# Two-layer graph attention on one core: the second layer's dense residual steps in two pieces for a node tile, in place of five

## The chip, the cores and the metric

The kernel runs on one core of a Trainium2 chip. A core has a matrix engine (TensorE; PE in the profile, its weight loads as PEld), a vector engine (VectorE, DVE), a scalar engine (ScalarE, ACT), GpSimd (POOL), a queue engine (SyncE, SP), and 16 DMA engines. The metric is the device time of one execution in microseconds (us). Three runs of the kernel before took 1968.49, 1970.66 and 1971.56 us; the median is 1970.66.

## The reference

The input is `x`, 3125 nodes by 768 features, and a graph of 53,125 edges (25,000 in each direction, and one from each node to itself), sorted by destination. A layer norm and a relu are followed by two graph attention layers and the sum with `x`:

```python
def gat_conv(x, edge_index, W, a_src, a_dst, bias, heads, out_ch, concat):
    xl = (x @ W).reshape(n, heads, out_ch)
    e = leaky_relu(alpha_src[src] + alpha_dst[dst], 0.2)
    alpha = softmax of e over the edges of each destination
    out = segment_sum(xl[src] * alpha[:, :, None], dst, num_segments=n)
    return out + bias
...
h0 = x
h = relu(layer_norm(gat_conv(h0, W1, 4 heads of 256))) + (h0 @ Wr1 + br1)
h1 = h
h = layer_norm(gat_conv(h1, W2, 1 head of 768))
h = h + (h1 @ Wr2 + br2)
return x + h
```

The change is in the second layer. Its sums over the edges (`segment_sum`) and its residual product `h1 @ Wr2 + br2` (1024 by 768) are worked on in one stage.

## The kernel before, in words

The nodes are cut into 25 tiles of 128 (the last has 53 rows). The edges of a node tile fill up to 17 slots of 128 edges. The function `sums` (L704) does the sums of a layer. For each node tile it goes through five rounds of 4, 4, 3, 3 and 3 slots. In a round, TensorE multiplies for each slot a weight tile `w` (edges by 32 destinations; the attention value where an edge ends at the destination) with the gathered rows `g` of that slot, and adds into the tile `pa` in PSUM (L830): sixteen recorded matmuls in a round, 32 columns wide, four groups of columns side by side. Then it issues the fetch of the next round: a gather for each slot on GpSimd's queue (L783, rows of layer 2's node table, into one of 26 buffers), a copy of three columns on ScalarE (L787), and `w` on VectorE (L805). After that comes `step(k)` (L715), where `k` counts the rounds from 0.

`step(k)` does two things. First it moves on each running `finish` generator (L726) of the node tiles before: the values `v`, `z` from `pa` (L753), the bias (L1396) and the norm's sums (L486) behind the second round of the next tile, the root on ScalarE (L492) behind the third, L496, L1399 and L1400 behind the fourth, and the store of the output (L1402) behind the fifth. L1400 reads the residual `xr`. Second it adds `pace[k]` to a balance, and calls `next(more)` once for every whole unit in it.

`more` is the dense work of the stage, the residual of node tiles 1 to 24 in order (`ahead_of`, L1340, calling `residual`, L1322; that of tile 0 stands ahead of the stage). For one node tile it has eleven steps. The first eight are two matmuls each into a pair of PSUM tiles `pr` (L1329, 128 by 128 by 384 in fp32; four matmuls in the trace's records), the first of them behind the loads of `h` and `xr` for the node tile two further on (L1309, L1319, SyncE's queue). The ninth is reached through the bias matmuls (L1333), two more are empty, and the call that starts the next node tile begins with VectorE's addition of `pr` into `xr` (L1338). Behind it, in the same call, stands that next tile's first pair of matmuls.

The order of the instructions on TensorE, ScalarE and VectorE is that in which the program writes them (`manual_schedule`, L814); a planner places those of GpSimd and SyncE. So what `pace` sets is after which round of `pa` how much of the dense work stands in TensorE's queue, and with it the additions on VectorE's and the loads on SyncE's.

The pace of layer 2 is one number for all five rounds:

```python
each = (NB - FIRST) * (NK2 + 3) / ((NB - 1.5) * len(ROUNDS))   # 24 * 11 / (23.5 * 5) = 2.2468
```

With it, two or three steps follow every round, 11.23 in a node tile. Over the stage, 62 rounds are followed by two pairs of matmuls, 16 by three, 20 by one and 27 by none (these meet the empty steps, or come when nothing is left); 108 rounds have dense matmuls behind them, the bias ones counted.

Of the kernel before, what the change touches and what calls it, by code (L numbers as in the profile page):

```python
# [33 lines left out]
ROUNDS = [(0, 5, 9, 13), (1, 6, 10, 14), (4, 11, 15), (2, 8, 16), (3, 7, 12)]  # L34
# [9 lines left out]
@with_exitstack  # L44
def preln_gat2_kernel(
    ctx: ExitStack,
    tc: tile.TileContext,
    x, src, dst,
    W1, a_src1, a_dst1, b1, g1, be1, Wr1, br1,
    W2, a_src2, a_dst2, b2, g2, be2, Wr2, br2,  # L50
    out,
):

    pool = ctx.enter_context(tc.tile_pool(name="flag", bufs=1))
    flag = pool.tile([1, 1], I32, name="flag")  # L60
    in_order(tc, x, src, dst, W1, a_src1, a_dst1, b1, g1, be1, Wr1, br1,
             W2, a_src2, a_dst2, b2, g2, be2, Wr2, br2, out, flag)
    other = tc.nc.values_load(flag[0:1, 0:1], min_val=0, max_val=1)
    with tc.If(other > 0):
        any_order(tc, x, src, dst, W1, a_src1, a_dst1, b1, g1, be1, Wr1, br1,
                  W2, a_src2, a_dst2, b2, g2, be2, Wr2, br2, out)
# [3 lines left out]
def in_order(  # L70
# [21 lines left out]
    C2 = W2.shape[1]  # L92
# [36 lines left out]
    table2 = dram.tile([N, C2], F32, name="table2")  # L129
# [51 lines left out]
    def bcast(vec, n, parts=P):  # L181
        return bass.AP(tensor=vec.tensor, offset=vec.offset, ap=[[0, parts], [1, n]])
# [11 lines left out]
    def store_rows(q, dst_, b, t):  # L194
        for o, e in pieces(b):
            q.dma_start(dst_[b * P + o:b * P + e, :], t[o:e])
# [284 lines left out]
    def norm_steps(pool, z, n, apart=1):  # L481
        f = n // 2
        P = z.shape[0]
        st = pool.tile([128, 2, 6], F32, name="bn_st")[:P]
        for i in range(2):
            nc.vector.bn_stats(st[:, i, :], z[:, i * f:(i + 1) * f])  # L486
        mv = pool.tile([128, 2], F32, name="bn_mv")[:P]
        nc.vector.bn_aggr(mv, st)  # L488
        for _ in range(apart):
            yield  # L490
        sd = pool.tile([128, 1], F32, name="bn_sd")[:P]
        nc.scalar.activation(sd, mv[:, 1:2], AF.Sqrt, bias=eps[:P])  # L492
        for _ in range(apart // 2 + 1):
            yield
        rstd = pool.tile([128, 1], F32, name="bn_rs")[:P]
        nc.vector.reciprocal(rstd, sd)  # L496
        norm_steps.found = mv[:, 0:1], rstd
# [348 lines left out]
    with tc.tile_pool(name="m1", bufs=1) as mp:  # L846
# [322 lines left out]
        with tc.tile_pool(name="w2", bufs=1, reuse_waits="tile") as wp, tc.tile_pool(name="e1", bufs=2, reuse_waits="tile") as ep, \  # L1169
# [14 lines left out]
            def later():  # L1184
                for i, members in enumerate(late_in):
                    n = cols_of(i)
                    held = [b for g in late_in[:i] for b in g]
                    while len([b for b in held if b not in gone]) + len(members) > 4:
                        yield
                    for b in members:  # L1190
                        made[b] = ep.tile([128, NK2, P], F32, name="r1l", bufs=4)
                    for m in range(NK2):
                        pm = pp.tile([128, 512], F32, name="pr", bufs=2)
                        for k in range(NK1):
                            nc.tensor.matmul(pm[:, :n], wr1[:, k, m * 128:(m + 1) * 128], loaded[i, k][:, :n],  # L1195
                                             start=(k == 0), stop=(k == NK1 - 1))
                            if m == NK2 - 1:
                                load(i + 1, k)
                            if k == NK1 - 1:
                                for t, b in enumerate(members):  # L1200
                                    r = rows_of(b)
                                    nc.scalar.activation(made[b][:, m, :r], pm[:, t * P:t * P + r], AF.Identity,
                                                         bias=br1_c[:, m:m + 1])
                                    if m == NK2 - 1:
                                        whole.add(b)
                            if k % 2:
                                yield

            more = later()
# [67 lines left out]
    with tc.tile_pool(name="m2", bufs=1, reuse_waits="tile") as mp, \  # L1277
            tc.tile_pool(name="pr2", bufs=1, space=PSUM, reuse_waits="tile") as pr:
        al2 = mp.tile([128, J, 1, NB], F32, name="al2")
        ends2 = mp.tile([128, J, NB, 3], F32, name="ends2")  # L1280
# [59 lines left out]
        def ahead_of(first, end, apart):  # L1340
            load(first)
            load(first + 1)
            for b in range(first, end):
                load(b + 2)
                yield from residual(b, apart)
# [40 lines left out]
        more = ahead_of(FIRST, NB, 3)  # L1386
        each = (NB - FIRST) * (NK2 + 3) / ((NB - 1.5) * len(ROUNDS))

        with tc.tile_pool(name="w3", bufs=1, reuse_waits="tile") as wp, tc.tile_pool(name="e2", bufs=2, reuse_waits="tile") as ep, \
                tc.tile_pool(name="g2", bufs=1, reuse_waits="tile") as gp, tc.tile_pool(name="pg2", bufs=1, space=PSUM, reuse_waits="tile") as pp:  # L1390
            with tc.issue_after(last_hot):
                nc.sync.dma_start(b2_b, bcast(b2, C2))
                nc.sync.dma_start(g2_b, bcast(g2, C2))

            def end2(b, z, share):
                nc.vector.scalar_tensor_tensor(z, z, share, b2_b[:z.shape[0]], op0=OP.mult, op1=OP.add)  # L1396
                yield from norm_steps(ep, z, C2, 1)
                mu, rstd = norm_steps.found
                nc.vector.scalar_tensor_tensor(z, z, mu, g2_b[:z.shape[0]], op0=OP.subtract, op1=OP.mult)  # L1399
                nc.vector.scalar_tensor_tensor(z, z, rstd, xrs[b][:z.shape[0]], op0=OP.mult, op1=OP.add)  # L1400
                yield
                store_rows(nc.scalar, out, b, z)  # L1402

            with tc.issue_after(behind), tc.issue_after(last_hot):
                sums(1, C2, table2, al2, ends2, 26, 1, gp, gp, pp, end2, more, [each] * len(ROUNDS))


@with_exitstack
# [469 lines left out]
```

## Time and profile before

| what | value |
|---|---|
| median of three runs | 1970.66 us |
| profiled execution | 1969.17 us |
| its span | 1967.3 us |
| granted TensorE clock, mean | 0.955 |
| busy, share of the span | PE 91%, PEld 50%, DVE 54%, POOL 46%, ACT 15% |
| stage of layer 2's sums | from 1344 us to some 1955 us of the span |

How to read it: busy is the time in which an engine has an instruction in work. PE and PEld overlap. L numbers are lines of the kernel. In lists of groups, what stands after a bar is the idle time of the engine just ahead of the group's instructions and what ended it; "issue" means that the profile shows nothing that was waited for. In the chain of waits, each row is a start, a length, and the work or wait that filled it. In tables by window the columns are busy us and count for each engine, the granted clock, the share of the DMA engines' time in use, and GB/s.

### The profile page before, as it was taken

What the parts mean: (1) busy time and instruction counts of PE and PEld (TensorE: products, weight loads), DVE (VectorE), ACT (ScalarE), POOL (GpSimd) and SP (SyncE); (2) the same over time, 40 slices, a digit from 0 to 9 for tenths busy, and PEclk for the clock granted to TensorE, in tenths of its full rate; (3) what the DMA queues carried; (4) which work ended last, traced back from release to release, by engine and by line L of the source; (5) the groups of instructions that cost most, each with busy time, mean ns of one, the idle gap of its engine ahead of it and who ended that gap; (6) DMA issues with size and microseconds to landing.
All of it is one profiled execution on the core that took longest, in us unless ns stands there. A gap on an engine that the chain in (4) does not pass through costs nothing. (4 is left out here: it accounts for less than half of the span.)

```text
span 1967.3 us, 34126 instructions
## 1 busy us (share of the span) xinstructions
PE 1794.7 (91%) x12558; PEld 986.9 (50%) x12558; DVE 1058.8 (54%) x3030; ACT 296.9 (15%) x1094; POOL 910.2 (46%) x991
## 2 busy tenths in 40 slices
PE   8999999998779999999999999869988898898896
PEld 5666665665446555565554554464333333333332
DVE  7673436986635566555665564344534444444445
ACT  2122331001202211221111121101100000000000
POOL 2000101112354666566666655134666666666662
PEclk9999999998889999999999998958989999999999
DMA  7834447775598999999999999576999999999984
GB/s 243 268 103 139 128 149 196 172 177 167 209 408 326 390 390 387 385 383 408 404 386 385 385 349 378 206 240 197 321 329 325 332 329 322 332 335 327 336 300 141
DMA packets 179889, 574.86 MB, mean 292 GB/s; under 512 B 32767, under 2 KB 55033, under 8 KB 179588
## 3 DMA queue, kind: packets, MB, share of 16 engines
q0 software_dynamic: 109552, 414.44, 59.1%
q1 hardware_dynamic: 65770, 147.77, 21.6%
q10 hardware_dynamic: 4394, 10.39, 1.3%
q8 instruction: 103, 1.69, 0.3%
q14 instruction: 70, 0.57, 0.1%
HBM read 503.27 MB, written 73.85 MB: 293 GB/s over the span
## 5 line engine op out<-in xcount | busy, mean ns | idle before, releaser
L783 POOL DMA_INDIRECT g<-table,idx_s x832 | 816.1, 981 | 557.4 <-issue 201.4
L830 PE MATMUL pa<-g,w 128*32 128x256 f32 (+2 forms) x5868 | 520.3, 433 | 61.2 <-issue 46.7
L830 PEld LDWEIGHTS pa<-g,w 128*32 128x32 f32 x5868 | 202.8, 111 | 344.5 <-issue 227.4
L1329 PE MATMUL pr<-wr,h 128*128 128x384 f32 (+1 forms) x800 | 304.6, 512 | 36.9 <-issue 34.5
L1264 PE MATMUL p<-w,h1T 128*128 128x384 f32 (+2 forms) x800 | 285.6, 504 | 4.9 <-DVE h1T L1250 2.6
L1329 PEld LDWEIGHTS pr<-wr,h 128*128 128x128 f32 (+1 forms) x800 | 144.0, 191 | 196.1 <-issue 130.1
L805 DVE TENSOR_SCALAR w<-iota_f,rel_s,al 128x32 f32<-128x32 f32 (+1 forms) x416 | 101.8, 314 | 254.8 <-PE pa L830 130.9
L1264 PEld LDWEIGHTS p<-w,h1T 128*128 128x128 f32 (+1 forms) x800 | 146.6, 190 | 130.3 <-issue 37.5
L810 DVE TENSOR_TENSOR w<-oh,al 128x128 f32<-128x128 f32 (+1 forms) x416 | 131.7, 317 | 118.3 <-PE pa L830 56.8
L935 PE MATMUL pm<-w,h0l 128*128 128x344 f32 (+1 forms) x468 | 142.5, 459 | 0.0
L1195 PE MATMUL pr<-h0k,wr 128*128 128x256 f32 (+1 forms) x576 | 140.9, 391 | 0.2
L1072 PE MATMUL pm<-h0g,wr 128*128 128x512 f32 x288 | 134.8, 617 | 0.0
L935 PE MATMUL pm<-w,h0g 128*128 128x344 f32 x432 | 130.0, 456 | 0.3 <-ACT h0g L914 0.3
L1195 PEld LDWEIGHTS pr<-h0k,wr 128*128 128x128 f32 x576 | 106.3, 190 | 30.5 <-issue 10.6
L1003 POOL DMA_DIRECT2D hot_d<-ohd x25 | 13.5, 539 | 218.8 <-DVE own L503 122.7
L809 DVE TENSOR_SCALAR oh<-iota_f,rel_s 128x32 f32<-128x32 f32 (+1 forms) x416 | 110.2, 265 | 0.5 <-issue 0.2
L935 PEld LDWEIGHTS pm<-w,h0l 128*128 128x128 f32 (+1 forms) x468 | 85.7, 187 | 44.9 <-issue 7.1
L492 ACT ACTIVATE bn_sd<-bn_mv,eps 128x1 f32<-128x1 f32 (+1 forms) x50 | 14.9, 297 | 617.3 <-DVE bn_mv L488 284.4
L935 PEld LDWEIGHTS pm<-w,h0g 128*128 128x128 f32 x432 | 81.4, 192 | 40.3 <-issue 0.9
L1072 PEld LDWEIGHTS pm<-h0g,wr 128*128 128x128 f32 x288 | 54.3, 197 | 59.2 <-issue 58.9
L1248 ACT ACTIVATE h1T<-p,be_c,g_c 128x128 f32<-128x128 f32 (+1 forms) x200 | 72.6, 480 | 20.0 <-PE p L1243 11.0
L554 DVE TENSOR_TENSOR scr<-pq,ohh 128x500 f32<-128x500 f32 x100 | 56.8, 596 | 29.1 <-PE pq L552 22.8
(306 smaller groups left out, 1434.1 us busy)
## 6 DMA issues: line engine op xcount, KB each, us to landing
s<-slo_d SPq DMA_DIRECT2D x25, 544.0 KB
g<-table,idx_s POOLq DMA_INDIRECT x832
table<-row SPq DMA_DIRECT2D x24, 512.0 KB
own<-table SPq DMA_DIRECT2D x24, 512.0 KB
h1T_d<-h1T SPq DMA_DIRECT2D x24, 512.0 KB
h<-h1T_d SPq DMA_DIRECT2D x22, 512.0 KB
ring<-in_x_dram SPq DMA_DIRECT2D x24, 384.0 KB
table<-row SPq DMA_DIRECT2D x24, 384.0 KB
```

Of the source, the lines that this page charges most:

```text
L554: nc.vector.tensor_tensor(pick[:, j0:j0 + n], q, ohh[:, j0:j0 + n, None, :].to_broadcast([128, n, heads, NB]), OP.mult)
L783: nc.gpsimd.indirect_dma_start(out=g[:, :width], out_offset=None, in_=table[:, :], in_offset=bass.IndirectOffsetOnAxis(ap=idx_s[:, b * J + ...
L805: nc.vector.tensor_scalar(w[:, 0, :], iota_f[:, lo:hi], rel_s[:, c:c + 1], al[:, POS[j], 0, b:b + 1], op0=OP.is_equal, op1=OP.mult)
L809: nc.vector.tensor_scalar(oh, iota_f[:, lo:hi], rel_s[:, c:c + 1], None, op0=OP.is_equal)
L810: nc.vector.tensor_tensor(w, oh[:, None, :].to_broadcast([128, heads, hi - lo]), al[:, POS[j], :, b:b + 1].to_broadcast([128, heads, hi - ...
L830: nc.tensor.matmul(pa[32 * q:32 * q + 32, o // f, o % f:o % f + m], w[:, o // cols, :], g[:, o:o + m], start=to not in opened, stop=False, ...
L935: nc.tensor.matmul(pm[:r, :C], h0[b][:, k, :], w1[:, k, i * C:(i + 1) * C], start=(k == 0), stop=(k == NK1 - 1))
L1072: nc.tensor.matmul(pm, wr1[:, k, m * 128:(m + 1) * 128], groups[gi][:, k, :], start=(k == 0), stop=(k == NK1 - 1))
L1195: nc.tensor.matmul(pm[:, :n], wr1[:, k, m * 128:(m + 1) * 128], loaded[i, k][:, :n], start=(k == 0), stop=(k == NK1 - 1))
L1248: nc.scalar.activation(hT[:, k0 + k, :r], pt[:, k, :r], AF.Relu, bias=be1_c[:, k0 + k:k0 + k + 1], scale=g1_c[:, k0 + k:k0 + k + 1])
L1264: nc.tensor.matmul(pm[:, :n], hT[:, k, :r], w2[:, k, o:o + n], start=(k == 0), stop=(k == NK2 - 1))
L1329: nc.tensor.matmul(pm[:, :384], h1[:, k, :r], wr2[:, k, i * 384:(i + 1) * 384], start=(k == 0), stop=False)
```

## The change

The pace that `sums` is given for layer 2 becomes nonzero for the second and the fourth round only:

```diff
-                sums(1, C2, table2, al2, ends2, 26, 1, gp, gp, pp, end2, more, [each] * len(ROUNDS))
+                sums(1, C2, table2, al2, ends2, 26, 1, gp, gp, pp, end2, more, (0, each * 5 / 2, 0, each * 5 / 2, 0))
```

Behind the second and behind the fourth round the balance grows by 5.617, so five or six steps follow each, and none follow the first, third and fifth. The sum for a node tile stays 11.23. Nothing is added or taken away: the same matmuls, additions, loads, gathers and weights are issued, in the same order within each kind. What differs is how the two streams of TensorE's matmuls are interleaved, and with them where VectorE's additions L1338 and SyncE's loads stand. Over the stage, 47 rounds have dense matmuls behind them.

## The prediction
> **What bounds the kernel now.** I read the page first: what ends last, and how busy TensorE is.
>
> ```profile
> span 1967.3 us, 34126 instructions
> ...
> PE 1794.7 (91%) x12558; PEld 986.9 (50%) x12558; DVE 1058.8 (54%) x3030; ACT 296.9 (15%) x1094; POOL 910.2 (46%) x991
> ...
> PE pr L1329 14%; PE pa L830 11%; PE pq L552 1%; DMA g<-table,idx_s 1%; PE pr L1333 1%; PE p L1264 1%; DMA pen<-near_d 1%; DMA hot<-hot_d 0%; POOL g L783 0%; DVE w L805 0%; DVE z L753 0%; DVE z L1396 0%; DVE bn_st L486 0%; PE pd L535 0%
> ```
>
> The two lines of the last stage, L1329 and L830, lead the chain that ended last. The view by window sets a stretch of layer 1's sums (first row) against layer 2's (second row); the columns are busy us of PE, PEld, DVE, ACT and POOL, granted clock, DMA share and GB/s.
>
> ```profile
> 860.00:1000.00 140.00, 139.21 (x1138) 82.69 (x1136) 83.33 (x277) 27.16 (x77) 86.87 (x91) 1.00 1.01 393
> 1400.00:1900.00 500.00, 442.15 (x2233) 175.60 (x2233) 221.71 (x677) 41.17 (x360) 328.06 (x332) 0.95 0.92 327
> ```
>
> PE is the busiest engine in layer 2 too (442 of 500), with DMA at 0.92, but 393 GB/s were had in layer 1, so DMA has room. The groups and the waits of 1340 to 1960 say what PE waits for.
>
> ```profile
> L783 POOL DMA_INDIRECT g<-table,idx_s x390 | 384.3, 985 | 211.7 <-issue 104.5 <-PE pa L830 53.5 <-remote 44.3
> L1329 PE MATMUL pr<-wr,h 128*128 128x384 f32 (+1 forms) x776 | 294.5, 510 | 36.9 <-issue 34.5 <-DMA g<-table,idx_s 1.6
> L830 PE MATMUL pa<-g,w 128*32 128x387 f32 (+1 forms) x1956 | 249.1, 521 | 33.3 <-issue 30.9 <-DVE w L805 1.2 <-PE pa L830 0.8
> L1329 PEld LDWEIGHTS pr<-wr,h 128*128 128x128 f32 (+1 forms) x775 | 138.9, 190 | 193.4 <-issue 129.3 <-DMA h<-h1T_d 0.6
> L805 DVE TENSOR_SCALAR w<-iota_f,rel_s,al 128x32 f32<-128x32 f32 (+1 forms) x416 | 101.8, 314 | 254.8 <-PE pa L830 130.9 <-remote 106.2 <-PE pr L1329 14.8
> L1338 DVE TENSOR_TENSOR xr<-pr,xr 128x384 f32<-128x384 f32 (+1 forms) x50 | 25.9, 551 | 75.4 <-remote 37.2 <-PE pa L830 29.9 <-PE pr L1333 6.5
> ```
>
> ```profile
> PE pr L1329 <- issue: 34.5, 52, 1.7
> PE pa L830 <- issue: 30.9, 61, 4.0
> ...
> PEld pa L830 <- DVE w L805: 9.2, 15, 1.9
> ```
>
> In the whole stage PE waits some 2 us for gathers and 10 us for weight tiles, and 65 us for nothing that is shown ("issue"). So it is bound by PE, and not by what feeds it.
>
> Then the chain of waits, for what PE's pieces cost. First a stretch that runs mostly clean: start, length, work.
>
> ```profile
> 1392.09 2.73 PE pa L830 x32
> 1394.82 2.78 PE pr L1329 x8
> ...
> 1401.65 2.78 PE pr L1329 x8
> 1404.43 1.43 PE pa L830 x16
> 1405.86 4.07 PE pr L1329 x12
> 1409.93 1.41 PE pa L830 x11
> 1411.41 0.51 PE pa L830
> 1412.14 1.56 PE pa L830 x4
> 1413.71 1.49 PE pr L1329 x4
> 1415.19 0.55 PE pr L1333 x2
> 1415.74 2.73 PE pa L830 x32
> ```
>
> One dense step (x4) takes 1.49 us, two 2.78, three 4.07. Each further step costs 1.29, so a block of them has a fixed price of 1.49 − 1.29 = 0.20 us. A round of `pa` takes 1.43, but two in a row 2.73, so an interruption costs 2 × 1.43 − 2.73 = 0.13. A dense block between two rounds hence costs 0.33 us beyond its work.
>
> Clean work would be 192 steps × 1.29 = 248, 125 rounds × 1.43 = 179, 24 bias pairs × 0.55 = 13 and 108 blocks × 0.20 = 22: 462 us. The stage lasts some 610. The rest is stalls and a lowered clock. The chain shows a stall (1517 to 1522), the windows a dip of the clock:
>
> ```profile
> 1511.05 4.07 PE pr L1329 x12
> 1515.12 1.43 PE pa L830 x16
> 1516.55 0.55 PE pr L1333 x2
> 1517.10 1.11 PE pa L830 x4
> 1518.21 0.25 issue
> 1518.47 0.49 PE pa L830
> 1518.96 0.92 issue
> 1519.88 0.52 PE pa L830 x2
> 1520.39 0.89 issue
> 1521.29 1.13 PE pa L830 x9
> 1522.42 1.49 PE pr L1329 x4
> ```
>
> ```profile
> 1425.00:1430.40 5.40, 1.52 (x4) 0.56 (x3) 1.01 (x5) 0.96 (x8) 4.12 (x5) 1.00 0.95 328
> 1430.40:1437.50 7.10, 5.11 (x19) 1.59 (x18) 2.52 (x6) 0.00 (x0) 3.45 (x4) 0.52 0.71 273
> ```
>
> The round at 1517.10 took 1522.42 − 1517.10 = 5.32 us where 1.43 is clean: 3.9 lost, one instruction at a time.
>
> **The change part by part.** *Fewer blocks.* 108 rounds have a dense block behind them before, 47 after: 61 blocks × 0.33 = 20.1 us less on the engine that sets the end. Of the blocks that go, about six hold the bias pair alone. That pair costs 0.55 us inside a block as well (1415.19, behind x4), so there only the interruption goes: 6 × 0.20 = 1.2 back. Eleven times a new residual's matmuls follow a bias pair without a round between. The trace has no such place; the price is between 0 (as the pair behind x4 costs no more) and a block's fixed 0.20. I take 0.20, as it is a new accumulation that starts: 2.2 back. Sum 20.1 − 1.2 − 2.2 = 16.7 us.
>
> *What of this lies in a stall.* A seam inside a stall costs nothing. By the chain from 1500 to 1560 about a third of the pieces are broken by stalls, so 16.7 holds if none of the removed seams is covered by one, and 16.7 × 2/3 = 11 if all of those are. I take the middle, 14.
>
> *The three rounds in a row.* The fifth round and the next tile's first two now follow each other, eleven gathers in some 3 × 1.37 = 4.1 us, with a burst of five or six steps (5.5 × 1.29 + 0.2 = 7.3 us) on either side. GpSimd issues a gather in 0.985 us, eleven in 10.8; PE takes 4.1 + 7.3 = 11.4 for these and the burst behind them. With 26 buffers, 1.5 tiles of gathers, this costs nothing; its cover is the lead of the gathers, which the 2 us of waits above show to be there. GpSimd, at 328 of 500 busy, must follow a stage 2% shorter: no cost. Eleven weight tiles are 11 × 0.314 = 3.5 us on VectorE, under the 4.1; twelve tile buffers hold them ahead, and VectorE's long operations on `z` stand behind the second round, where the burst covers them. Bound: 0 to the 10 us that PE waits for `w` now, once more; I take 0.
>
> *The additions L1338* move into the burst behind the fourth round, two of 0.551 on VectorE. Behind them wait three weight tiles of the next round, 0.9 us, beside at least one dense step (1.29) and two rounds in hand: nothing. Where the bias stands in the same block (eleven times), VectorE waits for it, at most the 7.3 us of the burst's remains; the 330 us in which VectorE waits for PE or for an unshown event ahead of L805 and L1338 already cost PE 10 us in all. *SyncE's loads* of `h` and `xr` move by at most two rounds, under 10 us, and stand two residuals (some 50 us) ahead; the one row with a wait for `h` has 0.6 us. *ScalarE's* copies and stores keep their rounds: 0.
>
> *Sum:* 1969.17 − 14 = 1955.2 in the profiled execution. The median of the runs lies 1.5 above that execution: 1956.7.
>
> **The clock.** Ahead of the dip above PE was busy 1.5 of 5.4 us at full clock, then had 0.52 for 7.1 us. The Trainium skill, "TensorE: Matmul & The Clock Gate", section "Part 1: The HAM clock gate", has the array fall to half clock after an idle window of some 3.4 us; the trace agrees, as the dip lasts about two such windows. By that rule a block that stalls for longer than a window would cost once more what follows it; the sum above would move only with the stalls, which I hold fixed.
>
> **The rivals.** *A, the stalls take it back.* The stalls are 610 − 462 = 148 us and nothing in the profile explains them. If something unseen paces the stage, a shorter PE programme only waits longer: no change, about 1970. For it: the rounds lose time with 65 us of "issue" and no releaser. Against: clean stretches such as 1392 to 1409 run at the price of their pieces alone.
>
> *B, slower: long blocks are followed by more stalls.* PE's queue is fed in order; after several short rounds in a row, or behind a long burst, the next instructions come late. For it: the block of three steps at 1405.86 is followed by a broken round, 1413.71 − 1409.93 = 3.8 us instead of 1.43. Against: the one at 1511.05 is followed by a clean round, and layer 1's stretch, whose pace too bunches its dense steps behind the first two rounds, is 139 of 140 us busy. Price: one more broken round costs 2.4 to 3.9 us, 3.1 between them; in half the 24 tiles, 12 × 3.1 = 37, less 14, is 23 slower, 1994; in a third, 1982. It decides from 14 / 3.1 = 5 more broken rounds in the stage on.
>
> *C, faster than the sum: the long burst hides the stall.* If the stall is a fixed delay that starts with a round's waits, 7.3 us of dense work ahead cover more of it than 2.8 do. One broken round less in a third of the tiles: 8 × 3.1 = 25, 14 + 25 = 39 less, 1932; in all tiles 1882, which GpSimd's 0.66 would not forbid, but nothing speaks for so much.
>
> **How the numbers follow.** The forecast, 1957 with a range of its own of 1950 to 1964 (20 to 7 us less, stalls unchanged), has 0.42. C, 1916 to 1949, has 0.12. A, within 0.2% (4 us, about what a measurement of this kernel can tell from no change), has 0.18. B, 1976 to 2000, has 0.28: one clear broken round speaks for it, one clean for the contrary, and PE's stalls are the part that I don't understand. So faster 0.54, same 0.18, slower 0.28. The range from 1936 to 1988 leaves out about half of C and a third of B.
>
> **What would show it.** Right: in the chain, blocks of x20 at 1.29 × 5 + 0.2 = 6.65 us, three rounds of `pa` in 4.1, and fewer rows; the "issue" idle time of L830 and L1329 still about 65 us. A shows as the same stage length with more "issue". B shows as broken rounds directly behind the bursts or in the second and third round of a row, or as waits of PEld for `w`; C as clean rounds behind the second round's burst. Wrong, too, if GpSimd's waits for PE fall to nothing and PE waits for gathers: then the feed is the bound.

## The result

The changed kernel took 1981.40 us (median of five runs, 1972.38 to 1983.73), the kernel before 1970.66 (five runs, 1968.49 to 1972.32). The ratio is 1.004, with an interval from 1.0021 to 1.006: the change makes the kernel slower by some 0.4%. The prediction was 1957, so the sign was wrong. The time lies in the range only because the range was drawn to take in rival B; the sum itself does not lead there. The profiled execution is the quickest of the five, 1972.38 against 1969.17 before, and shows 3 of the 11 us between the medians.

The page of the changed kernel, its span, busy times and chain:

```profile
span 1970.5 us, 34126 instructions
...
PE 1787.2 (91%) x12558; PEld 1001.4 (51%) x12558; DVE 1058.5 (54%) x3030; ACT 295.4 (15%) x1094; POOL 914.2 (46%) x991
```

PE's busy time falls by 1794.7 − 1787.2 = 7.5 us and the span grows by 3.2: TensorE has less to do and the kernel takes longer. The two ends of the stage, by the view of line L830, before:

```profile
L830 PEld LDWEIGHTS pa<-g,w x1956: 106/109/178, 1347.6 to 1953.8; 128*32 128x32 f32 x196
```

and after:

```profile
L830 PEld LDWEIGHTS pa<-g,w x1956: 106/110/178, 1344.8 to 1957.0; 128*32 128x32 f32 x196
```

The stage lasts 1957.0 − 1344.8 = 612.2 us, where it was 606.2. The chain of the changed kernel (start, length, work) has the pieces that were foreseen:

```profile
1404.54 2.87 PE pa L830 x29
1407.40 0.21 issue
1407.62 0.86 PE pa L830 x3
1408.47 1.81 PE pr L1329 x5
1410.28 0.34 issue
1410.63 1.22 PE pr L1329 x3
1411.85 0.55 PE pr L1333 x2
1412.40 4.02 PE pa L830 x48
1416.42 7.94 PE pr L1329 x24
1424.36 2.07 PE pa L830 x22
...
1427.31 0.50 PE pa L830
1427.80 0.92 issue
1428.72 0.48 PE pa L830
```

Three rounds in a row take 4.02 us and a burst of six steps 7.94 (6 × 1.29 + 0.20), close to what was worked out. But the rounds behind the burst at 1416.42 are broken. The groups from 1340 to 1965 say how much (what stands after the bar is idle time and what ended it):

```profile
L1329 PE MATMUL pr<-wr,h 128*128 128x384 f32 (+1 forms) x768 | 280.2, 509 | 25.0 <-issue 24.5
L830 PE MATMUL pa<-g,w 128*32 128x387 f32 (+1 forms) x1956 | 250.6, 521 | 51.1 <-issue 49.4 <-DVE w L805 0.9 <-DVE bn_mv L488 0.3
```

The dense steps stand idle for 25.0 us (36.9 before), the rounds for 51.1 (33.3 before), and the rounds' busy time has not fallen, though 61 interruptions are gone. The stalls went from the dense steps into the rounds, and grew from 70.2 to 76.1 us in all.

### The profile page after: what moved, and what is told of

Its sections match the earlier page's. It is cut to its first block, busy times and chain, and to the rows that moved or that the text cites. A ratio compares the mean times of both kernels' runs of the same rounds, so it can differ in the third digit from the quotient of the medians.

```text
span 1970.5 us, 34126 instructions
## 1 busy us (share of the span) xinstructions
PE 1787.2 (91%) x12558; PEld 1001.4 (51%) x12558; DVE 1058.5 (54%) x3030; ACT 295.4 (15%) x1094; POOL 914.2 (46%) x991
## 5 line engine op out<-in xcount | busy, mean ns | idle before, releaser
L830 PE MATMUL pa<-g,w 128*32 128x256 f32 (+2 forms) x5868 | 521.8, 434 | 77.9 <-issue 63.2
L830 PEld LDWEIGHTS pa<-g,w 128*32 128x32 f32 x5868 | 216.4, 112 | 362.7 <-issue 252.2
L1329 PE MATMUL pr<-wr,h 128*128 128x384 f32 (+1 forms) x800 | 293.3, 511 | 25.0 <-issue 24.5
L1264 PE MATMUL p<-w,h1T 128*128 128x384 f32 (+2 forms) x800 | 280.8, 497 | 4.5 <-DVE h1T L1250 2.6
L1329 PEld LDWEIGHTS pr<-wr,h 128*128 128x128 f32 (+1 forms) x800 | 149.2, 194 | 165.3 <-issue 90.5
L1338 DVE TENSOR_TENSOR xr<-pr,xr 128x384 f32<-128x384 f32 (+1 forms) x50 | 25.6, 548 | 110.8 <-PE pr L1329 33.2
```

The source lines that it names most:

```text
L830: nc.tensor.matmul(pa[32 * q:32 * q + 32, o // f, o % f:o % f + m], w[:, o // cols, :], g[:, o:o + m], start=to not in opened, stop=False, ...
L1264: nc.tensor.matmul(pm[:, :n], hT[:, k, :r], w2[:, k, o:o + n], start=(k == 0), stop=(k == NK2 - 1))
L1329: nc.tensor.matmul(pm[:, :384], h1[:, k, :r], wr2[:, k, i * 384:(i + 1) * 384], start=(k == 0), stop=False)
L1338: nc.vector.tensor_add(xr[:r, cs], pm[:, :384], xr[:r, cs])
```

## The experiments

The chips differ: on some the kernel before takes about 1968 us, on others about 1836. They are called the slower and the faster chip here, though each name stands for two chips or more. Each kernel was measured beside the kernel before on the same chip, and its ratio is to that. In brackets behind a ratio stands its 95% interval. The result above is from a slower chip.

### Does TensorE pace the stage?

One run leaves out every second pair of the residual's matmuls, the other leaves out four of seventeen gathers (and with them four of the small copies on ScalarE, L787):

```diff
                 for i, pm in enumerate(pms):
+                    if k % 2:
+                        continue
                     nc.tensor.matmul(pm[:, :384], h1[:, k, :r], ...
```

```diff
+                if heads == 1 and got and PLACE[j] in (3, 7, 10, 13):
+                    got[j] = got[max(got, key=lambda i: PLACE[i])][0], weights_of(b, j)
+                    continue
```

> The kernel before, with every second of the residual's eight pairs of matmuls left out (the odd k of L1329), so the residual is wrong; everything else stays. 96 pairs fewer at 1.29 us each is 124 us of TensorE's clean work. Theory P (TensorE paces layer 2's sums, its stalls are its own): at least 100 us faster than before, some 1850 to 1870, with stalls about as many. Theory F (the stage is paced by what feeds it, the gathers on GpSimd's queue, and TensorE's stalls are only slack being used up): a tile still takes about 25 us, faster by less than 40 us. Between 40 and 100: both bind in turn.

> The kernel before, with four of the seventeen gathers of a full tile in layer 2 left out (the slot takes the rows gathered for the slot before it, so the sums are wrong); TensorE's and VectorE's work stays, GpSimd's issues and the gathered bytes fall by 24%, and the 26 buffers reach two tiles ahead. Theory P: within 10 us of before, since TensorE's work is unchanged. Theory F: faster by 40 us or more (a tile of 25.5 us falls towards TensorE's clean 19 to 20).

Measured on the slower chip (before 1968.49): half the dense work 1957.95, ratio 0.9951 (0.9932 to 0.997); 13 of 17 gathers 1843.40, ratio 0.9351 (0.9317 to 0.9386). Taking 124 us of work from TensorE brings 10 us, and taking a quarter of the gathers, with TensorE's work unchanged, 125. PE's groups from 1400 to 1700, first before:

```profile
L1329 PE MATMUL pr<-wr,h 128*128 128x384 f32 x383 | 147.8, 514 | 21.2 <-issue 20.7
L830 PE MATMUL pa<-g,w 128*32 128x384 f32 (+1 forms) x931 | 117.6, 515 | 14.7 <-issue 14.7
```

then with half the dense work:

```profile
L830 PE MATMUL pa<-g,w 128*32 128x387 f32 (+1 forms) x956 | 156.2, 557 | 49.5 <-issue 46.0 <-ACT bn_sd L492 1.2 <-DVE w L805 1.1
L1331 PE MATMUL pr<-wr,h 128*128 128x384 f32 x200 | 86.8, 552 | 6.7 <-issue 6.1
```

and with 13 gathers:

```profile
L1332 PE MATMUL pr<-wr,h 128*128 128x384 f32 x495 | 177.3, 500 | 1.0 <-issue 1.0
L833 PE MATMUL pa<-g,w 128*32 128x387 f32 (+1 forms) x1196 | 121.2, 493 | 2.1 <-issue 2.1
```

The idle time without a releaser grows when TensorE has less to do (from 35.9 to 56.2 us) and all but vanishes when there are fewer gathers (3.1). It behaves as a wait for the feed, although the profile names none. The feed itself hardly changes: in these 300 us GpSimd issues 198 gathers before, 202 with half the dense work and 195 with 13 of 17. So the time goes with the number of gathers that there are to issue.

### Bytes or issues? VectorE?

```diff
-                    out=g[:, :width], out_offset=None, in_=table[:, :],
+                    out=g[:, n:width] if heads == 1 else g[:, :width], out_offset=None,
+                    in_=table.rearrange("a (t c) -> (a t) c", c=n)[:, :] if heads == 1 else table[:, :],
...
-                                             g[:, o:o + m], start=to not in opened, stop=False,
+                                             g[:, n:n + m] if heads == 1 else g[:, o:o + m], start=to not in opened, stop=False,
```

```diff
-                    own = owns[b] = ap.tile([128, width], F32, name="own", bufs=3)
-                    load_rows(nc.sync, own, table, b)
+                    if heads > 1 or b < 3:
+                        own = kept[b] = ap.tile([128, width], F32, name=f"own{b}" if heads == 1 else "own", bufs=1 if heads == 1 else 3)
+                        load_rows(nc.sync, own, table, b)
+                    owns[b] = kept[b % 3 if heads == 1 else b]
...
+                if b < 3:
...
+                    held[b] = h1, xr
+                xrs[b] = held[b % 3][1]
+                loaded[b] = held[b % 3]
```

```diff
-                nc.vector.scalar_tensor_tensor(z, z, share, b2_b[:z.shape[0]], op0=OP.mult, op1=OP.add)
-                yield from norm_steps(ep, z, C2, 1)
-                mu, rstd = norm_steps.found
-                nc.vector.scalar_tensor_tensor(z, z, mu, g2_b[:z.shape[0]], op0=OP.subtract, op1=OP.mult)
-                nc.vector.scalar_tensor_tensor(z, z, rstd, xrs[b][:z.shape[0]], op0=OP.mult, op1=OP.add)
+                yield
+                yield
+                nc.vector.scalar_tensor_tensor(z, z, share, xrs[b][:z.shape[0]], op0=OP.mult, op1=OP.add)
```

> The kernel before; every gather of layer 2 brings half a row (384 of 768 values), and both halves of the sums read it, so the sums are wrong. As many gathers, issues and instructions as before; 3.3 of 8.35 MB for a tile fall away. The runs so far show that the stage is paced by its feed. Theory B (the bytes: the DMA engines at some 335 GB/s): faster by about as much as with 13 of 17 gathers, 100 us or more, down to what TensorE's own work allows (about 1845). Theory I (the issue: the number of gathers that GpSimd issues): within 25 us of before.

> The kernel before without the loads of own, h and xr in layer 2 from the fourth node tile on (old contents are used again, so the output is wrong): 1.28 of 8.35 MB for a tile fall away (15%), the gathers stay. Theory B: 15% of a stage of 610 us, some 60 to 90 us faster. Theory I: within 20 us of before.

> The kernel before without layer 2's bias and norm (L1396, the norm's sums and root, L1399), some 5 us of VectorE for a tile; the output is wrong. Feed, TensorE's and DMA's work stay. Theory V (GpSimd's waits of some 4 us a tile come from VectorE's long operations, and these set the pace of the gathers): 40 us or more faster. Theory B: within 10 us of before.

These three were measured on the faster chip (before 1833.70), not on the one whose stalls were in question: half rows 1823.69, ratio 0.9938 (0.9914 to 0.9962); no loads 1827.09, 0.9958 (0.9945 to 0.9971); no norm 1827.24, 0.9966 (0.9948 to 0.9984). Bytes, loads and VectorE's norm are worth 0.3 to 0.6% each there; nothing near 40 us. With half rows GpSimd issues 233 gathers in 300 us there at a DMA share of 0.76 (the columns are busy us of PE, PEld, DVE, ACT and POOL, clock, DMA share, GB/s):

```profile
1400.00:1700.00 300.00, 287.01 (x1607) 121.45 (x1607) 156.17 (x476) 28.52 (x252) 229.29 (x233) 0.99 0.76 233
```

Before, as shown in the next section, it issues 232 at a share of 1.00, so the full DMA engines do not set the rate there. Two of the three were run again on the slower chip (before 1967.08):

> Half rows in layer 2's gathers once more (as many gathers, 40% fewer bytes; the sums are wrong). On the chip with 1834 us it brought 10 us, and its profile had GpSimd issuing without a pause. Where before takes about 1969: theory B (bytes: 335 GB/s is this chip's ceiling for these gathers): 100 us or more faster. Theory I (the rate at which gathers are issued): within 25 us of before, GpSimd's waits still some 0.25 us a gather.

> Layer 2 without the loads of own, h and xr once more (15% of its bytes; the output is wrong). Where before takes about 1969: theory B 60 to 90 us faster, theory I within 20 us.

Half rows 1960.68, ratio 0.9966 (0.995 to 0.9983); no loads 1959.68, 0.9964 (0.9947 to 0.9981). Theory B falls. With half rows the window reads

```profile
1400.00:1700.00 300.00, 263.35 (x1353) 107.43 (x1353) 131.05 (x399) 24.47 (x216) 193.38 (x200) 0.96 0.67 200
```

beside before's

```profile
1400.00:1700.00 300.00, 264.57 (x1338) 104.62 (x1338) 132.15 (x403) 24.70 (x216) 195.06 (x198) 0.96 0.92 328
```

The DMA share falls from 0.92 to 0.67, and GpSimd issues 200 gathers in 300 us in place of 198. What paces the stage is the number of gathers, not their bytes. The norm was left out on the faster chip only.

### The faster chip

```diff
-... more, [each] * len(ROUNDS))
+... more, (0, each * 5, 0, 0, 0))
```

(one piece for a tile; the other two are the kernels before and after the change.)

> The kernel before once more, for its profile on the chip of this job. Two chips have shown two times of it, some 1969 and some 1834 us. Theory C (chips differ in how fast layer 2's gathers are fed): where the time is about 1834, the profile shows TensorE above 97% busy in layer 2's sums, the chain without issue rows, and tiles of 20 to 21 us; where it is about 1969, tiles of 25.5 us with broken rounds, as in the first profile.

> The change once more. Where the kernel before takes about 1834 us and TensorE paces the stage, the seams count: 12 to 20 us faster than before (1814 to 1822). Where it takes about 1969, the feed paces the stage and the change is 4 to 15 us slower, as it was.

> One piece a tile once more. Where before takes about 1834: as TensorE paces, the seams alone would make it 18 to 28 us faster than before; if the bunching starves TensorE of gathers (26 buffers, eleven or more releases while a burst of 15 us runs), no faster than the change. Where before takes about 1969: 50 to 65 us slower, as it was.

On the faster chip (before 1837.10) the kernel before, run once more, took 1835.09; the change 1837.49, ratio 0.9993 (0.9974 to 1.0012); one piece 1838.30, ratio 1.0003 (0.9981 to 1.0024). The pace makes no difference, and theory C is half wrong: TensorE does not pace the stage there either, at 288.77 of 300 us busy. The kernel before on this chip, window and chain:

```profile
1400.00:1700.00 300.00, 288.77 (x1600) 120.50 (x1592) 156.55 (x480) 28.51 (x252) 228.40 (x232) 0.99 1.00 384
```

```profile
1506.47 7.45 DMA g<-table,idx_s
...
1513.99 0.95 POOL g L783
1514.94 0.31 issue
1515.25 8.32 DMA g<-table,idx_s
1523.56 0.14 issue
1523.70 1.49 PE pa L830 x12
1525.19 2.78 PE pr L1329 x8
1527.97 0.78 PE pa L830 x6
```

Here the chain runs through the gathers, and TensorE's rounds are clean between waits for them. GpSimd's list shows its rhythm on this chip (start, busy, idle ahead of it):

```profile
1501.46 0.94 POOL L783 DMA_INDIRECT g<-table,idx_s  x1 [0.30 <-issue]
1502.71 0.95 POOL L783 DMA_INDIRECT g<-table,idx_s  x1 [0.30 <-issue]
1503.96 0.95 POOL L783 DMA_INDIRECT g<-table,idx_s  x1 [0.31 <-issue]
```

and on the slower chip, the kernel before of the first profile:

```profile
1516.25 0.94 POOL L783 DMA_INDIRECT g<-table,idx_s  x1 [0.30 <-issue]
1517.49 0.94 POOL L783 DMA_INDIRECT g<-table,idx_s  x1 [0.30 <-issue]
1518.74 0.94 POOL L783 DMA_INDIRECT g<-table,idx_s  x1 [0.30 <-issue]
1521.75 0.94 POOL L783 DMA_INDIRECT g<-table,idx_s  x1 [2.07 <-remote]
```

A gather occupies GpSimd for 0.95 + 0.30 = 1.25 us, and seventeen are 21.3 us for a tile. Over the window a gather takes 300 / 232 = 1.29 us on the faster chip, close to that floor, and 300 / 198 = 1.52 on the slower one, where pauses such as the 2.07 us above stand between. The view of line L830 has the stage from 1304.3 to 1819.3 on the faster chip, 515.0 us where the slower one takes 606.2. GpSimd's idle time ahead of the stage's 390 gathers is 131.0 us there and 211.7 here: 81 of the 91 us between the stages. Another 43 us of the chips' difference lie ahead of the stage, which begins at 1347.6 on the slower chip.

The pause shown falls into TensorE's stall from 1517.10 to 1522.42, which the prediction shows, but that is not the rule. By the lists of both engines, GpSimd pauses 27 times for more than 0.8 us between 1400 and 1700, 50 us in all, and 12 of TensorE's 35 idle us lie inside these pauses. With 13 of 17 gathers GpSimd stands idle as long (106.4 us ahead of 195 gathers, 103.9 ahead of 198 before), while TensorE's 3.1 us are left. So the two need not stop together, and what GpSimd waits for is not shown.

### The price of a seam

The cut to 13 gathers and the change's pace together:

> 13 of 17 gathers together with the change's pace (0, each*5/2, 0, each*5/2, 0); the sums are wrong in the same way as in the run with 13 of 17 gathers, 1843 us, which it is compared with. There TensorE is 98% busy and paces the stage. If the price of a seam (0.33 us for each of 61 blocks, less the corrections) was right and only the stage's bound was read wrong, it is 12 to 20 us faster than that run, 1823 to 1831. If long blocks cost TensorE something of their own, it is not faster.

> 13 of 17 gathers with the pace of before, the twin of the run with 13 of 17 gathers and the change's pace (1762 us). Where before takes about 1834: TensorE paces both kernels, 1772 to 1785, so that the change's pace is worth 12 to 20 us there, too; if it is 1765 or less, the seams are worth little even where TensorE paces. Where before takes about 1969: 1843 again.

On the faster chip 13 of 17 gathers took 1781.54 with the pace of before, ratio 0.968 (0.9648 to 0.9712), and 1761.65 with the pace of the change, ratio 0.9604 (0.9565 to 0.9644). By the ratios the change's pace is worth 0.0076 × 1836 = 14 us there (4 to 24 by the intervals), by the medians 20. TensorE is 300.00 of 300 us busy in both, first with the pace of before, then with that of the change:

```profile
1400.00:1700.00 300.00, 300.00 (x1804) 130.01 (x1796) 174.70 (x539) 26.19 (x217) 202.66 (x205) 1.00 0.97 359
1400.00:1700.00 300.00, 300.00 (x1870) 142.89 (x1866) 183.29 (x562) 27.86 (x231) 215.11 (x214) 1.00 0.98 370
```

GpSimd issues 205 and 214 gathers in the window, fewer than the 232 that it reaches on this chip, so TensorE is what ends last. The view of line L833, which is L830 in these kernels, has the stage from 1307.3 to 1767.7 and from 1303.1 to 1746.2 us: 460.4 and 443.1, 17.3 less. So the 16.7 us of the sum agree with the price of the seams where TensorE paces.

> 13 of 17 gathers with the change's pace once more (the sums are wrong). Where before takes about 1969, its twin with the pace of before took 1843: if the seam price holds wherever TensorE paces, 1823 to 1833; if long blocks cost something on that chip, 1840 or more. Where before takes about 1834: 1762 again, 20 below its twin.

On the slower chip it was 1852.67, ratio 0.941 (0.9384 to 0.9436), not below its twin's 0.9351 (0.9317 to 0.9386). The seams bring nothing there even with fewer gathers; the rounds stall again, 7.1 us where the twin has 2.1:

```profile
L1332 PE MATMUL pr<-wr,h 128*128 128x384 f32 x484 | 167.8, 495 | 0.7 <-issue 0.5
L833 PE MATMUL pa<-g,w 128*32 128x384 f32 (+1 forms) x1200 | 121.5, 490 | 7.1 <-issue 6.9
```

The number of gathers offers a reason. GpSimd issues 193 of them in these 300 us and 195 in the twin, no more than the 198 of the kernel with all seventeen. At 300 / 195 = 1.54 us each, thirteen take 20.0 us, above the 19 us that a tile's clean work takes on TensorE. So the feed seems to pace the stage even then, although TensorE is recorded as 97 and 99% busy. No run on the slower chip left out more gathers, so this is not shown.

### Where the pieces stand, and buffers

```diff
-... more, [each] * len(ROUNDS))
+... more, (each * 5 / 2, 0, each * 5 / 2, 0, 0))
```

> The pace (each*5/2, 0, each*5/2, 0, 0): two pieces for a tile as in the change, one round earlier each. If it is the number of pieces that costs, as the change (about 1981). If it is the place (VectorE's work on z and the norm, emitted behind the second and the fourth round, standing beside or away from the bursts), nearer to 1970 or further away than 1990.

> The pace (0, each*5, 0, 0, 0): all of a tile's eleven or twelve dense steps behind its second round. About 24 blocks where the change has 47 and the kernel before 108. If clean seams were what counts: some 7 us faster than the change. If bunching itself costs (longer runs of short rounds, burst of 15 us): slower than the change, 1985 to 2010. If the stage is paced from elsewhere: within 5 us of the change.

> The change once more, to pair it with before on one chip. Where before takes about 1969: 4 to 15 us slower. Where about 1834: within 4 us.

On the slower chip, pieces behind the first and third round took 1968.68, ratio 1.0003 (0.9985 to 1.0021); one piece 2027.03, ratio 1.0292 (1.0264 to 1.0321); the change once more 1973.26 against 1967.08, ratio 1.0038 (1.0021 to 1.0055), which agrees with the first measurement. First and third have as many blocks as the change, and as long ones, and lose nothing. So it is neither the number of blocks nor their length alone. PE's groups of that run from 1400 to 1700:

```profile
L1329 PE MATMUL pr<-wr,h 128*128 128x384 f32 x388 | 134.7, 497 | 0.4 <-issue 0.4
L830 PE MATMUL pa<-g,w 128*32 128x384 f32 (+1 forms) x944 | 122.5, 523 | 40.4 <-issue 31.2 <-DVE w L805 5.8 <-DMA g<-table,idx_s 1.8
```

Almost all stalls are in the rounds, and the kernel takes as long as before. So stalls that moved into the rounds, as those of the change did, need not cost anything.

What sets the change apart from first and third is open; two things were compared. One is the clock: 0.96 in this window before and with first and third, 0.93 and 0.92 in the two profiles of the change, 0.93 with one piece. But over the whole stage it is 0.95 with first and third, which loses nothing, and 0.95 and 0.94 with the change; and with half the dense work it is 0.86, at 10 us less. The other is GpSimd's row. Its 390 gathers in the stage keep it busy 384.3 us before and 384.6 with first and third, and 389.9 and 391.7 in the two profiles of the change. The 6 to 7 us have the size of the loss, but the idle time ahead of the gathers varies as much (211.7, 214.3, 214.7 and 207.3 in the same order), and what would lengthen a gather is not shown. With one piece the loss does stand in that idle time, 266.9 us ahead of 392 gathers, and 190 gathers are issued in the window.

```diff
-sums(1, C2, table2, al2, ends2, 26, 1, ...
+sums(1, C2, table2, al2, ends2, 20, 1, ...
```

> The kernel before with 20 gather buffers in layer 2, where it has 26. If GpSimd is never short of a free buffer (its gathers are issued a median of some 7 us after their buffer was released), six buffers fewer cost nothing: within 5 us of before. If free buffers are what its gaps wait for, slower by 10 us or more.

> The change with 20 gather buffers. In the change, buffers come free in bunches: eleven within three rounds, none in a burst of 7 us. If that is how the change costs time (GpSimd runs out of free buffers in a burst), the loss grows with fewer buffers: 15 us or more slower than the run with 20 buffers and the pace of before. If the loss is as with 26 (0 to 9 us), buffers are not its cause.

On the faster chip (before 1838.63): 20 buffers 1845.32, ratio 1.0034 (1.0018 to 1.0051); 20 buffers with the change 1848.58, ratio 1.0043 (1.0024 to 1.0062). Six buffers cost some 7 us, and the change's pace some 3 beside that, where the intervals overlap. For the slower chip, where the change loses, the question stays open.

## Why the prediction was wrong

**What bounds the kernel: wrong, and the step that failed.** The prediction read "it is bound by PE, and not by what feeds it" off two small waits, 2 us for gathers and 10 for weight tiles, and held 148 us of stalls fixed, so that seams saved on TensorE would shorten the stage. On the slower chip the runs with half the dense work (10 us) and with 13 gathers (125 us) show that the stalls fill what the number of gathers leaves. TensorE busy 442 of 500 us, with idle time that has no releaser, did not show a bound.

**The feed's price: mis-sized.** GpSimd was put at 0.985 us a gather, its busy time. The same row's idle column, 211.7 us of which 104.5 "issue", belongs to the price: 1.25 us is the floor, 21.3 us for a tile, above TensorE's clean 19 (462 / 24). With that term the feed would have been the bound on both chips, and a sum over TensorE's seams worth nothing. The floor explains the faster chip's 1.29 us; on the slower one the pauses bring a gather to 1.52, or 25.8 us for seventeen. The rival of a feed that binds was only named as a last way to be wrong, with no chance of its own.

**The seams: right as a price.** Blocks of 6.65 and 7.94, three rounds in 4.02, 14 to 20 us by the runs with 13 gathers on the faster chip (17.3 by their stages), against 16.7. One term was a little off: stepping the pace through the kernel's code gives ten blocks that hold the bias pair alone before and none after, not about six, which makes the sum 15.9.

**Rival A** had the right mechanism: the stalls took the gain back. On the faster chip that is the whole result, 0.9993; on the slower one a loss of 0.4% comes on top, which A did not foresee. **Rival B** had the sign and a sight that came true, broken rounds behind the bursts; but its reason, that a long block itself causes a stall, is not borne out, as the pieces behind the first and third round are as long and cost nothing. **Rival C** is contradicted: long bursts hid nothing.

**The clock** moved, as the paragraph on it allowed: 0.93 after, 0.96 before in the same window. That paragraph says that the trace agrees with an idle window as the cause of a dip. The length of the dip fits, but ahead of it TensorE was busy 1.52 of 5.40 us and never idle for more than 1.66, so the trace shows no such window. By the whole stage's 0.95 and 0.96 (two digits only), an estimate from these figures is (0.05 × 612 − 0.04 × 607) × 2 = 13 us more at half clock, which would cost at most 6 us of clean work. That is about the 6 us by which the stage grew, but first and third has the same 0.95 and loses nothing, and no run held the clock fixed. So the clock is not shown to be the cause.

What stays open is what makes GpSimd pause on the slower chip, and why the places behind the second and fourth round cost 0.4% there.

## What to carry to other kernels

A busy engine with idle time that no releaser explains is not shown to be the bound; the quickest test is to take work from it and, in another run, from its feed. Price an issuing engine by the distance between its instructions, not by their busy time. A saving on an engine counts only once the feed has room, which 13 gathers show on the faster chip: the same edit is worth 14 to 20 us with them and nothing without.

## What the runs showed of the hardware

The same kernel took 1836 us on some chips and 1968 on others, with the same clean pieces (1.43, 2.78, 4.07 us) and the same 1.25 us from one gather to the next where they follow without a pause. In the stage of layer 2's sums most of the difference (81 of 91 us) is idle time of GpSimd ahead of its gathers. On the slower chip these pauses did not depend on the bytes moved: 200 GB/s with half rows and 328 before gave 200 and 198 gathers in 300 us. A profile of one chip alone would not have told that most of these pauses are absent on another.
